# Summing a head's sixteen products by identity matmuls on TensorE for two of a block's full pairs of chunks

## Chip, cores, metric

One NeuronCore of one Trainium2 chip runs the whole program. The metric is the time on the device in microseconds, from one launch. All arithmetic of the kernel is in fp32. In the text PE is TensorE, DVE is VectorE, ACT is ScalarE, POOL is GpSimd and SP is SyncE, which issues plain DMAs.

## What is computed

Sixteen graphs share one sparse adjacency matrix of 1024 nodes (about 0.8% of its entries are ones). A node has 128 features for each graph. Four layers run one after the other: three of attention with eight heads of 16 features (L0, L2, L3), and one graph-attention layer with a single head (L1). Cut to what matters here, an attention layer is:

```
Q = (h @ Wq).reshape(B, N, NUM_HEADS, HEAD_DIM)     # 8 heads of 16
K = (h @ Wk).reshape(B, N, NUM_HEADS, HEAD_DIM)
V = (h @ Wv).reshape(B, N, NUM_HEADS, HEAD_DIM)
scores = einsum('bnhd,bmhd->bhnm', Q, K) / sqrt(HEAD_DIM)
scores = where(adj_matrix == 0, -inf, scores)
attn = softmax(scores, axis=-1)
attn_out = einsum('bhnm,bmhd->bnhd', attn, V).reshape(B, N, OUT_DIM)
x = layer_norm(h + (attn_out @ Wo + bo))
y = relu(x @ W1 + b1) @ W2 + b2
x = layer_norm(x + y)
```

The change concerns the sum over d in `scores`, the product of a query and a key over the 16 features of a head.

## The kernel before

**Sparse form.** Nodes are sorted by degree. For a set of 128 edge slots, K and V rows of the neighbours are gathered from a table in HBM, one row of each slot to a partition, 8 graphs at a time. Such a set is a chunk: 128 slots, 8 graphs x 128 features of K (`ROW` = 1024 numbers), and as many of V.

**Units, pieces, parts.** A unit is a layer, a half of the graphs (`GR` = 2) and a block of 128 nodes (`T` = 8); an attention layer has 16 units, the kernel 48 of them, and L1 has 16 of its own. A unit's chunks stand in pieces of two (full pairs) and one piece of a single mixed chunk, which is always the fourth of the unit (`MIX`). Blocks 1 to 6 have four full pairs, block 0 has five and block 7 has three. In the attention layers each piece is one part, the step of the main loop.

**The work of a part,** and its lines:

- `gathered` (L942, POOL): two indirect DMAs bring K and V rows into one of four buffers `e`.
- `products` (L954, DVE): K times the queries, elementwise, into `pr` (128 x 2048), one of four buffers.
- `exponentials` (L977, DVE): a reduction over the 16 features of each head, 128 x 2048 to 128 x 128, into `sc`; then the exponential `ex` (L981, ACT).
- `weighted` (L1005, DVE): V times `ex`, into the same `pr`. When it has read V, the gather buffer is free, and the gather four parts ahead is issued.
- `summed` (L1021, PE): matmuls with 0/1 matrices `marks` add the slots of each node into the accumulator `acc`.

When a unit is done, `divided` (L1058, L1061) divides by the sum of the exponentials, and `attention_tail` (L697 to L739) does the rest of the layer for the two halves of the graphs: transposes (L642), Wo (L706), W1 (L717), W2 (L731), the additions of the residual by the matrix `centre` (L707, L735) and two normalisations (L620, L635 on ACT). `project` (L572, L576) makes the next layer's table. `queries` (L896 to L908) makes the next unit's queries and spreads them over the slots.

**The order is written by hand.** Each engine runs its instructions in the order of the program. In step i the loop emits `products(i)`, `summed(i-2)`, a round of other work (`others`: steps of the tails, queries, loads), `exponentials(i)`, in a unit's second part also the copies of the shared queries (`shared`, on SP) and the loading of a later unit's inputs (`loaded`), a second round of `others`, `weighted(i-1)`, the gather of part i-1+4, and a third round. PSUM tiles named `ps` take turns in four banks (`bank`).

Of the kernel before, what the change touches and what calls it, by code (L numbers as in the profile page):

```python
# [17 lines left out]
AF = mybir.ActivationFunctionType  # L18
# [4 lines left out]
P = 128  # L23
D = 128
H = 8
HD = 16
# [19 lines left out]
G = B // GR  # L46
# [20 lines left out]
MIX = J  # L67
# [44 lines left out]
def of_piece(v, piece):  # L112

    a, b = piece[0][0], piece[-1][0]
    if len(piece) == 2 and a == b:
        return v[:, a : a + 1].to_broadcast([v.shape[0], 2, v.shape[2]])
    return v[:, a : b + 1 : max(b - a, 1)]
# [20 lines left out]
def sparse_path(ctx: ExitStack, tc: tile.TileContext, a: dict, out: bass.AP, flag):  # L138


    nc = tc.nc
# [6 lines left out]
    def bank(shape):  # L148
        return banks.tile(shape, F32, tag="ps", name="ps")

    ident = const.tile([P, P], F32, name="ident")
# [50 lines left out]
    def gather_buffer():  # L202
        return gathers.tile([P, max(4 * ROW, J * (ROW + G))], F32, tag="e", name="e")
# [618 lines left out]
    def exponents():  # L822
        return exps.tile([P, MOST * G * H], F32, tag="ex", name="ex")
# [3 lines left out]
    parts = []  # L827
# [7 lines left out]
    es, prs, exs, qs, qx, ofs, accums = {}, {}, {}, {}, {}, {}, {}  # L835

    def is_attention(u):
        return LAYERS[units[u][0]][1] is ATTN
# [122 lines left out]
    def exs_of(i):  # L961

        u, pieces = parts[i]
        t = units[u][2]
        c, n = PLACE[(t, *pieces[0][0])], sum(map(len, pieces))
        return exs[u][:, c : c + n, :], n

    def exponentials(i):
        u, pieces = parts[i]
        t = units[u][2]  # L970
        heads = H if is_attention(u) else 1
        sc = smalls.tile([P, es[i].shape[1], G * heads], F32, tag="sc", name="sc")
        if u not in exs:
            exs[u] = exponents()[:, : MOST * G * heads].rearrange("p (c a) -> p c a", a=G * heads)
        ex, n = exs_of(i)
        if is_attention(u):
            nc.vector.tensor_reduce(  # L977
                sc[:, :n, :], prs[i][0][:, :n, :].rearrange("p k (a d) -> p k a d", d=HD),
                mybir.AxisListType.X, ALU.add,
            )  # L980
            nc.scalar.activation(ex, sc[:, :n, :], AF.Exp, scale=1.0 / HD**0.5)  # L981
        else:
            k = 0
            for piece in pieces:
                m = k + len(piece)
                nc.vector.tensor_tensor(
                    sc[:, k:m, :], es[i][:, k:m, ROW:], of_piece(ofs[u], piece), ALU.add
                )
                k = m
            nc.vector.scalar_tensor_tensor(  # L990
                sc[:, :n, :], sc[:, :n, :], SLOPE, sc[:, :n, :], ALU.mult, ALU.max
            )
            nc.scalar.activation(ex, sc[:, :n, :], AF.Exp)
# [88 lines left out]
    def advance(gens):  # L1082
        for gen in list(gens):
            got = next(gen, "end")
            if got == "end":
                gens.remove(gen)
            elif got == "free":
                free.append(gen)
# [3 lines left out]
    def idle():  # L1092
        return slow if held[0] or not busy[0] else []

    def others():
        pace[0] += pace[1]
        while pace[0] >= 1.0:
            advance(tails)
            pace[0] -= 1.0
        while True:  # L1100
            gens = fronts or loads or idle()
            if not gens:
                break
            got = next(gens[0], "end")
            if got == "end":
                gens.pop(0)
                continue
            if got == "idle":
                advance(idle())
            break  # L1110

    with tc.manual_schedule():
        wide = [gather_buffer() for _ in range(EDGES)]
        setup, entry, weights = graph(wide), at_once(0), load_weights("L0")
        next(setup)
        next(weights)
        next(entry)
        more = [weights, load_graph_weights()]
        rest = slots()
        for i, room in enumerate(setup):  # L1120
            if i == T:
                for gen in more:
                    next(gen)
            if room == "load":
                for _ in loaded(0):
                    next(entry, None)
            elif room == "queries":
                for _ in entry:
                    pass
                for _ in queries(0):  # L1130
                    pass
            elif isinstance(room, str):
                next(rest)
            else:
                for _ in range(room):
                    next(entry, None)
        for _ in entry:
            pass
        scratch.close()
        prods = ctx.enter_context(tc.tile_pool(name="prods", bufs=4))  # L1140
        smalls = ctx.enter_context(tc.tile_pool(name="smalls", bufs=3))
        slow.append(at_leisure(1))
        second = loaded(1)
        next(second)
        for i in range(AHEAD - 1):
            gathered(i)
        nc.gpsimd.memset(wide[3], 0.0)
        gathered(AHEAD - 1)
        fronts.extend([islice(rest, 4), second] + more)
        closing, sizes = None, ()  # L1150
        begun = 0
        for i in range(len(parts) + 2):
            here = i < len(parts)
            u = parts[i][0] if here else len(units)
            if here:
                l = units[u][0]
                if i and parts[i - 1][0] != u:
                    begun = i
                    if u < T - 1:
                        fronts.append(islice(rest, 4))  # L1160
                    if l + 1 < len(LAYERS) and LAYERS[l + 1][1] is ATTN:
                        if units[u][1:] == (0, 1):
                            more = load_weights(LAYERS[l + 1][0])
                            next(more)
                            next(more)
                        if units[u][1:] == (0, 4):
                            fronts.append(more)
                if is_attention(u):
                    products(i)
            if i > 1:  # L1170
                summed(i - 2)
                done = parts[i - 2][0]
                if parts[i - 1 : i] == [] or parts[i - 1][0] != done:
                    closing = divided(done)
                    next(closing)
            others()
            if here:
                exponentials(i)
            if here and i == begun + 1:
                if is_attention(u):  # L1180
                    shared(u)
                while loads:
                    advance(loads)
                if u + 1 < len(units):
                    fronts.append(queries(u + 1))
                loads.append(loaded(u + 2))
                if u:
                    advance(loads)
            others()
            if 0 < i <= len(parts):  # L1190
                weighted(i - 1, 0)
                if not is_attention(parts[i - 1][0]):
                    others()
                    weighted(i - 1, 2)
                gathered(i - 1 + AHEAD)
                for _ in sizes:
                    pass
            if closing is not None and here:
                while any(gen not in free for gen in tails):
                    advance(tails)  # L1200
                next(closing)
                sizes, closing = closing, None
                passes = 3 if is_attention(u) else 4
                steps = STEPS if is_attention(done) else GRAPH_STEPS
                steps -= LATE[units[done][0]]
                pace[:] = 0.0, steps / (passes * sum(part[0] == u for part in parts) - 1)
            others()
            if i + 1 >= len(parts) or parts[i + 1][0] != u:

                while fronts:  # L1210
                    advance(fronts)
        while tails:
            advance(tails)
        for _ in closing:
            pass
        while tails:
            advance(tails)
# [11 lines left out]
    ps = bank([1, 1])  # L1229
# [423 lines left out]
```

## Time and profile before

| what | value |
|---|---|
| runs, us | 2286.37, 2286.7, 2300.34; median 2286.7 |
| span of the profiled execution | 2290.8 us |
| PE / DVE / ACT / POOL busy | 90 / 82 / 67 / 46% |
| reductions L977 of 128 x 2048 | 192, 438.9 us, 2286 ns each |
| `products` L954 of 128 x 2048 | 192, 439.7 us, 2290 ns each |
| exponentials L981 of 128 x 128 | 192, 61.9 us, 323 ns each |
| DMA, mean | 278 GB/s |

The first attention unit is closed at 162 us and the last at 2253 us; the units of L1 lie between 793 and 1060 us. A group of instructions is shown as: line, engine, operation, output and inputs with shapes, count, then busy us and the mean of one in ns, and after the second bar the idle time of the engine just before it and what ended that. For PE the duration of one matmul contains the time in which the next is already under way.

### The profile page before, as it was taken

The numbers are of one execution on the slowest core, as the hardware profiler recorded it, in microseconds if no ns is written. First come the engines' busy times: TensorE is split into PE (matmuls) and PEld (weight loads), VectorE is DVE, ScalarE is ACT, GpSimd is POOL, SyncE is SP. The second block draws the span as 40 slices with busy tenths as digits, with TensorE's granted clock in tenths as the row PEclk, the third lists the DMA queues.
The fourth block names the chain that finished last, engine by engine and source line by source line (L and its number), as shares of the span: only waits on it lengthen the run. The fifth ranks groups of instructions, "written<-read, shape, count | busy, mean of one in ns | idle before, by whom it ended". The sixth has DMA issues, their size and how long they took to land. (4 is left out here: it accounts for less than half of the span.)

```text
span 2290.8 us, 36572 instructions
## 1 busy us (share of the span) xinstructions
PE 2052.0 (90%) x13140; PEld 1271.6 (56%) x13140; DVE 1871.1 (82%) x1472; ACT 1530.3 (67%) x5041; POOL 1050.7 (46%) x730
## 2 busy tenths in 40 slices
PE   6479999899998999998899989999999988998987
PEld 5336666555555555554465655655655555555544
DVE  7898888588888477777988889988888887988783
ACT  3237777777776565556677777777777766776765
POOL 3355344245445278884443434333344444444540
PEclk8789999999999999999999999999999998999999
DMA  7868888678887699997998978888887877677750
GB/s 249 278 217 300 304 279 305 240 247 302 285 295 265 197 330 354 354 373 288 326 318 292 319 254 306 296 314 295 281 282 277 291 258 250 242 275 270 260 217 20
DMA packets 165197, 636.06 MB, mean 278 GB/s; under 512 B 35064, under 2 KB 37880, under 8 KB 116510
## 3 DMA queue, kind: packets, MB, share of 16 engines
q0 software_dynamic: 89216, 485.08, 59.3%
q1 hardware_dynamic: 75792, 148.57, 18.9%
q8 instruction: 105, 1.72, 0.3%
q14 instruction: 84, 0.69, 0.1%
HBM read 581.08 MB, written 92.34 MB: 294 GB/s over the span
## 5 line engine op out<-in xcount | busy, mean ns | idle before, releaser
L942 POOL DMA_INDIRECT e<-table,idx x576 | 844.2, 1466 | 1022.1 <-DVE pr L1005 796.6
L1005 DVE TENSOR_TENSOR pr<-e,ex 128x2048 f32<-128x2048 f32 (+1 forms) x320 | 661.3, 2075 | 55.9 <-ACT ex L981 32.7
L954 DVE TENSOR_TENSOR pr<-e,qr 128x2048 f32<-128x2048 f32 x192 | 439.7, 2290 | 160.3 <-DMA e<-table,idx 91.5
L1021 PE MATMUL acc<-pr,marks 128*32 128x512 f32 x2624 | 528.5, 616 | 20.3 <-DVE pr L1005 16.4
L977 DVE TENSOR_REDUCE sc<-pr 128x128 f32<-128x2048 f32 (+1 forms) x240 | 497.5, 2073 | 8.0
L620 ACT ACTIVATE z<-yps,root 128x128 f32<-128x128 f32 x888 | 319.0, 390 | 35.6 <-PE yps L735 16.8
L1021 PEld LDWEIGHTS acc<-pr,marks 128*32 128x32 f32 x2624 | 108.7, 111 | 280.9 <-issue 231.6
L635 ACT ACTIVATE z<-yps,rstd 128x128 f32<-128x128 f32 x888 | 255.0, 371 | 7.2
L731 PE MATMUL yps<-W,f 128*128 128x128 f32 x1520 | 252.6, 283 | 7.7 <-ACT f L726 1.9
L726 ACT ACTIVATE f<-ps,b 128x512 f32<-128x512 f32 x190 | 130.6, 695 | 160.4 <-PE ps L717 159.7
L731 PEld LDWEIGHTS yps<-W,f 128*128 128x128 f32 x1520 | 205.7, 193 | 51.7 <-issue 26.2
L572 PE MATMUL ps<-Wkv,xT 128*128 128x256 f32 x768 | 212.2, 417 | 20.0 <-ACT xT L648 14.4
L908 ACT COPY qr<-ps 128x512 f32<-128x512 f32 x384 | 197.1, 602 | 47.7 <-PE ps L905 47.7
L642 PE MATMUL ps<-ident,z 128*128 128x128 f32 x896 | 179.7, 300 | 41.4 <-ACT z L635 36.6
L642 PEld LDWEIGHTS ps<-ident,z 128*128 128x128 f32 x896 | 116.2, 143 | 167.7 <-ACT z L635 86.5
L717 PE MATMUL ps<-x,W 128*128 128x512 f32 x384 | 193.9, 630 | 12.5 <-ACT x L650 12.4
L620 ACT ACTIVATION_READ_ACCUMULATOR z<-yps,root 128x1 f32 x888 | 203.7, 229 | 0.0
L905 PE MATMUL ps<-q,rep 32*128 32x512 f32 x768 | 166.5, 661 | 36.4 <-ACT q L900 34.0
L572 PEld LDWEIGHTS ps<-Wkv,xT 128*128 128x128 f32 x768 | 146.5, 204 | 73.9 <-ACT qr L908 18.0
L981 ACT ACTIVATE ex<-sc 128x128 f32<-128x128 f32 (+1 forms) x240 | 76.4, 318 | 157.9 <-DVE sc L977 157.8
L576 ACT COPY kv<-ps 128x512 f32<-128x512 f32 x176 | 103.3, 593 | 108.1 <-PE ps L572 85.8
L706 PE MATMUL yps<-Wo,oT 128*128 128x128 f32 x768 | 159.9, 291 | 10.0 <-ACT oT L648 10.0
(174 smaller groups left out, 2724.2 us busy)
## 6 DMA issues: line engine op xcount, KB each, us to landing
table<-kv SPq DMA_DIRECT2D x88, 512.0 KB
kept<-xT SPq DMA_DIRECT2D x96, 256.0 KB
x<-kept SPq DMA_DIRECT2D x48, 512.0 KB
qx<-qr SPq DMA_DIRECT2D x48, 256.0 KB
e<-table,idx POOLq DMA_INDIRECT x576
table<-kv SPq DMA_DIRECT2D x32, 256.0 KB
qx<-qr SPq DMA_DIRECT2D x18, 384.0 KB
qx<-qr SPq DMA_DIRECT2D x42, 128.0 KB
```

The lines of the kernel that those rows point to most:

```text
L572: nc.tensor.matmul(ps[:, k, :], x[:, i + k, :], w[LAYERS[l][0], "Wkv"], start=True, stop=True,)
L620: nc.scalar.activation(z[:, i, :], y[:, i, :], AF.Square, scale=D**-0.5, bias=root, accum_out=total[:, i : i + 1],)
L635: nc.scalar.activation(z[:, i, :], y[:, i, :], AF.Copy, scale=rstd[:, i : i + 1])
L642: nc.tensor.transpose(ps[:, i, :], z[:, i, :], ident)
L717: nc.tensor.matmul(ps, p["W1"][:, f * P : (f + 1) * P], x1.rearrange("p g n -> p (g n)"), start=True, stop=True,)
L731: nc.tensor.matmul(ps[:, i, :], f1[:, f, i * P : (i + 1) * P], p["W2"][:, f, :], start=(f == 0), stop=False,)
L908: nc.scalar.copy(qs[u][:, j, h * GH * D : (h + 1) * GH * D], pss[j])
L942: nc.gpsimd.indirect_dma_start(out=es[i][:, k, :], out_offset=None, in_=tables[l, g][:, :], in_offset=bass.IndirectOffsetOnAxis(ap=idx[:, ...
L954: nc.vector.tensor_tensor(prs[i][0][:, :n, :], es[i][:, :n, :ROW], qx[u].rearrange("p (o c) -> p o c", o=1) if (MIX, 0) in piece else of_p ...
L977: nc.vector.tensor_reduce(sc[:, :n, :], prs[i][0][:, :n, :].rearrange("p k (a d) -> p k a d", d=HD), mybir.AxisListType.X, ALU.add,)
L1005: nc.vector.tensor_tensor(prs[i][k0 // 2][:, :m, :].rearrange("p k (a d) -> p k a d", d=d), es[i][:, k0 : k0 + m, base : base + ROW].rearr ...
L1021: nc.tensor.matmul(outs[32 * j : 32 * j + 32], marks[:, mark, :], rhss, start=(chunk == mine[0]), stop=(chunk == mine[-1]),)
```

## The change

In an attention unit, the parts at positions 1 and 4 (counted from 0), where they are full pairs, no longer reduce on DVE. `by_matmul` picks them. For such a part sixteen matmuls with the identity as stationary matrix read `pr`, each taking the numbers at one feature d of all heads (every 16th number of a row), and add them up in one PSUM tile of 128 x 128. ACT takes the exponential from there. The tile `sc` is not written for these parts. Their call of `exponentials` is emitted after the second round of `others` instead of before it.

```diff
+    def by_matmul(i):
+
+        u, (piece, *_) = parts[i]
+        if not is_attention(u) or (MIX, 0) in piece or len(piece) < 2:
+            return False
+        first = next(k for k in range(i, -1, -1) if k == 0 or parts[k - 1][0] != u)
+        return i - first in (1, 4)
+
     def exponentials(i):
...
-        if is_attention(u):
+        if by_matmul(i):
+            ps = bank([P, n, G * H])
+            terms = prs[i][0][:, :n, :].rearrange("p k (a d) -> p k a d", d=HD)
+            for d in range(HD):
+                nc.tensor.matmul(
+                    ps, ident, terms[:, :, :, d], start=(d == 0), stop=(d == HD - 1)
+                )
+            nc.scalar.activation(ex, ps, AF.Exp, scale=1.0 / HD**0.5)
+        elif is_attention(u):
             nc.vector.tensor_reduce(
...
-            if here:
+            if here and not by_matmul(i):
                 exponentials(i)
             if here and i == begun + 1:
                 if is_attention(u):
...
             others()
+            if here and by_matmul(i):
+                exponentials(i)
             if 0 < i <= len(parts):
                 weighted(i - 1, 0)
```

## The prediction

> **What bounds the kernel now.** I read the busy table first, then the sums of busy time over stretches, then single instructions in order of time.
>
> ```profile
> PE 2052.0 (90%) x13140; PEld 1271.6 (56%) x13140; DVE 1871.1 (82%) x1472; ACT 1530.3 (67%) x5041; POOL 1050.7 (46%) x730
> L942 POOL DMA_INDIRECT e<-table,idx x576 | 844.2, 1466 | 1022.1 <-DVE pr L1005 796.6
> L954 DVE TENSOR_TENSOR pr<-e,qr 128x2048 f32<-128x2048 f32 x192 | 439.7, 2290 | 160.3 <-DMA e<-table,idx 91.5
> L977 DVE TENSOR_REDUCE sc<-pr 128x128 f32<-128x2048 f32 (+1 forms) x240 | 497.5, 2073 | 8.0
> ```
>
> GpSimd waits 797 us for VectorE (L1005 frees the gather buffers), which makes VectorE look like the engine to relieve. But its own idle time names others. The stretches below lie inside L0, inside L1, over L2 and inside L3; columns are PE, weight loads, VectorE, ScalarE and GpSimd busy us, granted clock, DMA share, GB/s.
>
> ```profile
> 162.00:756.00 594.00, 545.32 (x3604) 352.74 (x3603) 489.07 (x373) 438.34 (x1488) 268.10 (x183) 0.99 0.80 279
> 790.00:1060.00 270.00, 259.50 (x1839) 145.82 (x1841) 189.24 (x239) 158.29 (x597) 190.73 (x138) 0.99 0.92 340
> 1105.00:1700.00 595.00, 559.35 (x3553) 351.73 (x3551) 521.60 (x301) 441.30 (x1410) 237.86 (x162) 0.97 0.85 295
> 1700.00:2224.00 524.00, 471.95 (x2989) 284.38 (x2986) 445.89 (x249) 371.70 (x1204) 242.54 (x165) 0.95 0.74 265
> ```
>
> TensorE is the busiest in every stretch; VectorE follows at 82, 88 and 85% in the attention layers. [...]I count spacing in the order of time (start, duration, instruction):
>
> ```profile
> 1309.57 0.61 PE L731 MATMUL yps<-W,f 128*128 128x128 f32 x4
> 1310.02 0.39 PE L735 MATMUL yps<-centre,x 128*128 128x128 f32 x2
> 1310.24 0.61 PE L731 MATMUL yps<-W,f 128*128 128x128 f32 x4
> 1310.69 0.39 PE L735 MATMUL yps<-centre,x 128*128 128x128 f32 x2
> ```
>
> The reader is to see that four instructions take 0.45 us from start to start and two take 0.22: **110 ns per 128x128 fp32 instruction**, although one is shown as 275 ns long. I count 512-column instructions at 430 ns from L717's starts in the same view (1307.65 to 1308.08). One L2 unit, 1289.45 to 1326.13 (36.7 us), then holds: 120 instructions of 128 columns (13.2 us), 16 of L905 and 24 of L572 at 215 ns (8.6), four blocks of L1021 at 1.72 (6.9), 8 of L717 (3.4) and the small sums (0.9): 33.0 us, **90% real load**. The same count over 500:700 (L0) gives 170 of 200 us (85%), over 1700:2200 (L3) 404 of 500 (81%). In L2 VectorE's waits name PE (the accumulations of L1021 21.8 us, others 15 us) ahead of the gathers (13 us); only in L3 do gathers lead (62.8 us). So TensorE sets the pace in L2 and is close behind in L0 and L3.
>
> [...]L745 issues 32 calls and shows 64 matmuls, so a call is two instructions. [...]loads overlap here, and 110 ns contains them. [...]The change reads every 16th fp32, 64 bytes apart[...]. No TensorE read of that kind is in the trace. VectorE has one (L271, 128 elements 128 bytes apart, 365 ns) against 279 ns for 128 adjacent ones (L474), some 0.7 ns more for each element.
>
> **The change, part by part.** How often: eight units of 128 rows in each of two graph groups in three attention layers; seven have two such pairs, the last (three pairs) has one. That is 15 x 2 x 3 = 90 parts, 30 a layer.
>
> *Removed:* 90 reductions at 2.286 us from VectorE, 205.7 us or 4.3 us a unit.
>
> *Added:* 90 bursts of 16 calls, 32 instructions each. At 110 ns a burst is 3.52 us; 2880 instructions are **316.8 us** on TensorE, 105.6 a layer, 6.6 a unit. Weight loads: the same 2880, inside the 110. Lower end for one instruction: 110 ns, since nothing of this form runs faster here[...]. Upper end: VectorE's extra 0.7 ns on 128 elements gives 200, rounded to a doubling, 220 ns; then the bursts are 634 us. I take 110: an fp32 element is needed only every 0.86 ns here[...]; VectorE's is an inference across engines.
>
> *ScalarE:* the exponential reads PSUM instead of SBUF. L908 and L900 read PSUM at 0.60 us for 512 columns, so 128 columns stay near the present 0.32. Between nothing and 0.1 us each, 9 us in all; ScalarE is 67% busy, nothing if so covered.
>
> *Moved:* for these parts the exponential goes behind `shared`, `loaded` and a second round of other work. Passed on SP are the copies qx<-qr (1 to 3) and one load of kept; on POOL in L0 the row gathers. They read nothing the exponential makes, so they start no later. The gather of the next part still waits for `weighted`. On ScalarE the tail's copies of that round now go ahead of the exponential; `weighted` of the next step needs it, behind one earlier `weighted` and one `products` (4.6 us), enough for a 3.5 us burst unless PE is behind. Where PE is behind, it is PE's own time, counted already.
>
> *New waits:* the burst stands in PE's queue until `products` is done. Ahead of it are an accumulation (about 1.8 us) and two rounds of other matmuls, against 2.29 us of `products`, so the wait is near nothing; from 0 to 1 us a burst, 90 us at worst. Behind it stand the tails and the next accumulation. The burst takes one of four banks until its exponential; one eviction late costs about 0.6 us, 0 to 50 us in all. Neither gain nor loss is taken for these.
>
> **The sum.** Real load a unit plus 6.6 against the present length: L0 0.855 x 39.6 + 6.6 = 40.5 (now 39.6); L2 0.90 x 37.0 + 6.6 = 39.9 (now 37.0); L3 0.81 x 37.8 + 6.6 = 37.2 (now 37.8). A perfectly packed TensorE would add 0.9, 2.9 and 0 us, x16 = 61 us: the lower bound, 2350. If every bubble stays, all 317 come on top: 2608. I take 93% packing, between L2's 90% and the 96% that L1 shows: 43.5, 42.9, 40.0 us, so +3.9, +5.9, +2.2, x16 = +192. The profiled span is 2290.8, 0.2% above the median 2286.7; 2483 of span is **2480 us** as a median. The removed 205.7 us of VectorE are worth nothing here: TensorE then covers them, and what is late next is the accumulation L1021 and whatever PE does behind a burst.
>
> **The rivals.**
> *1. Strided reads cost a doubling.* [...]Against: TensorE's slow fp32 pace. Per unit 13.2 us: 47.1, 46.5, 43.8, over 0.95 (a fuller queue) 49.6, 48.9, 46.1, so +10.0, +11.9, +8.3, x16 = +483: about 2770. Between the two, any partial penalty.
> *2. VectorE is the bound and the burst is hidden: faster.* The place is PE's idle time in the stretches above, 48.7 + 35.6 + 52.0 = 136 us, 3.0 a unit. It decides where a burst is under half of that, 1.5 us or 47 ns per instruction. For it: GpSimd's 797 us wait on VectorE, and the page's large VectorE share. Against: 110 ns spacing. The gathers' own queue is 74 to 85% busy, so I price half of the 206: 2185.
> *3. It costs as much as it gives.* L0 and L3 hide all, L2's ScalarE waits vanish: 2287 to 2310.
> *4. The change does less than it says,* if identity weights stayed loaded and each call ran as one pass: 16 x 110 = 1.76 us a burst, 3.3 a unit; with half of the 3.0 idle absorbed +1.8 x 48 = +86, still slower, 2375.
>
> **How the numbers follow.** Forecast 0.50 (its own range 2350 to 2608), rival 1 and partial penalties 0.38, rival 2 0.05, rival 3 0.03, rival 4 0.04. A measurement of this kernel tells about 1% (23 us) from no change. Faster over 1%: 0.05. Within 1%: 0.03. Slower: 0.92. The range leaves out rivals 2 to 4 and the far ends, and takes in rival 1's price: 2375 to 2790.
>
> **What will show it.** Starts of consecutive identity matmuls 110 ns apart (rival 1: nearer 220). PE near 95% busy in L2, VectorE from 88% to under 72%. VectorE's waits on PE and on the exponential grow to hundreds of us. GpSimd's wait for L1005 stays, since slots come free no sooner. L2 grows most, L3 least. I am wrong if identity matmuls are spaced under 50 ns, if VectorE stays above 85% with a shorter span, or if PE's idle time grows: then the burst's waits, not its length, are the price.

## The result and the profile after

The changed kernel takes 2782.8 us (median of 4 runs, 2777.0 to 2785.9) against 2291.6 us before: a ratio of 1.2145, interval 1.2103 to 1.2187. It is slower, as forecast, but by 491 us and not by 193; the price is that of the first rival (2770 us), not of the forecast (2480 us, at most 2608 with every idle gap kept).

The page of the changed kernel, busy table and groups (line, engine, operation, count, busy us, mean ns, then idle time before and its releaser). L988 is the identity matmul, L1021 is `weighted`, L1037 the accumulation, L991 the exponential from PSUM, L993 the reductions that remain:

```profile
PE 2628.4 (94%) x16020; PEld 1843.6 (66%) x16020; DVE 1683.7 (60%) x1382; ACT 1528.1 (55%) x5041; POOL 1029.7 (37%) x730
...
L942 POOL DMA_INDIRECT e<-table,idx x576 | 837.7, 1454 | 1514.5 <-DVE pr L1021 1283.9
L1021 DVE TENSOR_TENSOR pr<-e,ex 128x2048 f32<-128x2048 f32 (+1 forms) x320 | 666.1, 2090 | 610.3 <-ACT ex L991 492.2
L988 PE MATMUL ps<-pr,ident 128*128 128x128 f32 x2880 | 644.1, 395 | 14.2 <-DVE pr L954 10.3
...
L954 DVE TENSOR_TENSOR pr<-e,qr 128x2048 f32<-128x2048 f32 x192 | 438.8, 2285 | 229.4 <-PE acc L1037 163.2
...
L991 ACT ACTIVATE ex<-ps 128x128 f32<-128x128 f32 x90 | 24.9, 277 | 558.4 <-PE ps L988 558.4
L993 DVE TENSOR_REDUCE sc<-pr 128x128 f32<-128x2048 f32 (+1 forms) x150 | 291.7, 1945 | 5.1
```

The counts are as worked out: 2880 instructions on PE, 90 reductions gone (240 to 150). PE's busy time rose by 576 us, DVE's fell by 187. The bursts (the sixteen matmuls of a part, 32 instructions) are busy 644 us, but the span grew by 493 only: PE's idle time fell by 83 us (239 to 156), and its other instructions were busy 68 us less (1984 instead of 2052). The mean granted clock of the profiled execution was 0.979 after and 0.956 before; what that is worth in time was not tried. DVE now waits for the exponential of these parts (492 us) and ACT for the bursts (558 us), but PE itself waited for `products` only 10 us before a burst: the queue is behind because PE is full. Stretches inside L2 and L3 (columns as before):

```profile
1300.00:2050.00 750.00, 735.82 (x4430) 533.80 (x4430) 447.57 (x262) 433.01 (x1378) 220.55 (x158) 1.00 0.67 231
2050.00:2740.00 690.00, 675.24 (x4087) 477.82 (x4086) 415.24 (x238) 395.62 (x1292) 247.91 (x170) 1.00 0.60 207
```

PE is 98% busy in both, at a granted clock of 1.00, DVE 60%. One burst in order of time, on PE:

```profile
1520.84 1.88 PE L717 MATMUL ps<-x,W 128*128 128x512 f32 x4
1522.56 7.14 PE L988 MATMUL ps<-pr,ident 128*128 128x128 f32 x32
1529.63 1.91 PE L1037 MATMUL acc<-pr,marks 128*32 128x512 f32 x8
```

From its start to the next instruction's start a burst takes 7.07 us, 221 ns for each of its 32 instructions, and not 110. The mean time from one unit's closing to the next (starts of the reciprocal after each unit; in L0 from its first to its last, in the other layers from the last of the layer before to their own last) shows where it went:

| us per unit | before | after | forecast | rival 1 | adjacent reads |
|---|---|---|---|---|---|
| L0 | 39.6 | 51.9 | 43.5 | 49.6 | 45.0 |
| L1 | 19.4 | 19.3 | unchanged | unchanged | 19.0 |
| L2 | 36.8 | 47.0 | 42.9 | 48.9 | 40.9 |
| L3 | 37.4 | 46.1 | 40.0 | 46.1 | 39.7 |

The last column belongs to the first experiment.

### The profile page after: what moved, and what is told of

The parts are those of the page before. It is cut to its first block, busy times and chain, and to the rows that moved or that the text cites. A ratio compares the mean times of both kernels' runs of the same rounds, so it can differ in the third digit from the quotient of the medians.

```text
span 2784.1 us, 42319 instructions
## 1 busy us (share of the span) xinstructions
PE 2628.4 (94%) x16020; PEld 1843.6 (66%) x16020; DVE 1683.7 (60%) x1382; ACT 1528.1 (55%) x5041; POOL 1029.7 (37%) x730
## 5 line engine op out<-in xcount | busy, mean ns | idle before, releaser
L1021 DVE TENSOR_TENSOR pr<-e,ex 128x2048 f32<-128x2048 f32 (+1 forms) x320 | 666.1, 2090 | 610.3 <-ACT ex L991 492.2
L988 PE MATMUL ps<-pr,ident 128*128 128x128 f32 x2880 | 644.1, 395 | 14.2 <-DVE pr L954 10.3
L988 PEld LDWEIGHTS ps<-pr,ident 128*128 128x128 f32 x2880 | 587.5, 207 | 58.9 <-issue 11.7
L1037 PE MATMUL acc<-pr,marks 128*32 128x512 f32 x2624 | 514.1, 604 | 14.6 <-DVE pr L1021 11.4
L991 ACT ACTIVATE ex<-ps 128x128 f32<-128x128 f32 x90 | 24.9, 277 | 558.4 <-PE ps L988 558.4
L993 DVE TENSOR_REDUCE sc<-pr 128x128 f32<-128x2048 f32 (+1 forms) x150 | 291.7, 1945 | 5.1
L1037 PEld LDWEIGHTS acc<-pr,marks 128*32 128x32 f32 x2624 | 107.0, 110 | 255.3 <-issue 219.6
L572 PE MATMUL ps<-Wkv,xT 128*128 128x256 f32 x768 | 203.1, 403 | 7.0 <-ACT xT L648 4.3
L642 PE MATMUL ps<-ident,z 128*128 128x128 f32 x896 | 173.4, 295 | 12.1 <-ACT z L635 6.3
L572 PEld LDWEIGHTS ps<-Wkv,xT 128*128 128x128 f32 x768 | 140.9, 196 | 57.8 <-ACT qr L908 19.5
```

The lines of the kernel that those rows point to most:

```text
L572: nc.tensor.matmul(ps[:, k, :], x[:, i + k, :], w[LAYERS[l][0], "Wkv"], start=True, stop=True,)
L642: nc.tensor.transpose(ps[:, i, :], z[:, i, :], ident)
L988: nc.tensor.matmul(ps, ident, terms[:, :, :, d], start=(d == 0), stop=(d == HD - 1))
L993: nc.vector.tensor_reduce(sc[:, :n, :], prs[i][0][:, :n, :].rearrange("p k (a d) -> p k a d", d=HD), mybir.AxisListType.X, ALU.add,)
L1021: nc.vector.tensor_tensor(prs[i][k0 // 2][:, :m, :].rearrange("p k (a d) -> p k a d", d=d), es[i][:, k0 : k0 + m, base : base + ROW].rearr ...
L1037: nc.tensor.matmul(outs[32 * j : 32 * j + 32], marks[:, mark, :], rhss, start=(chunk == mine[0]), stop=(chunk == mine[-1]),)
```

## The experiments

Three causes could double a burst: the step of the reads (theory S), weight loads that do not overlap with the matmuls (W), sixteen additions waiting for each other on one PSUM tile (A). Beside them stood the late exponential, and the worth of the freed DVE.

**Adjacent reads.** Sizes, weights, accumulation and order stay:

```diff
-                    ps, ident, terms[:, :, :, d], start=(d == 0), stop=(d == HD - 1)
+                    ps.rearrange("p k a -> p (k a)"), ident, flat[:, d * P : (d + 1) * P],
+                    start=(d == 0), stop=(d == HD - 1),
```

> The sixteen identity matmuls of a burst read 128 adjacent numbers of pr each instead of every 16th; number, sizes, weights and the one accumulating PSUM tile stay. It sums other products than a head's sixteen, so the scores are not the reference's. Theory S (the step of 64 bytes between elements of the moving operand costs the doubling): the instructions come 110 ns apart, a burst takes 3.5 us instead of 7.1, and the time is what the forecast gave for an undoubled burst, 2480 us (2350 to 2608). Theory W (the repeated loads of the identity do not overlap with the matmuls, 110 + 110) and theory A (sixteen additions on one PSUM tile wait for each other): 221 ns, 7.1 us and 2780 us stay.

Measured: 2469.9 us, ratio 1.0824 (1.0785 to 1.0864). The group and, from the order of time, one burst:

```profile
L988 PE MATMUL ps<-pr,ident 128*128 128x128 f32 x2880 | 339.3, 276 | 9.9 <-DVE pr L954 9.9
```

```profile
1413.66 3.73 PE L988 MATMUL ps<-pr,ident 128*128 128x128 f32 x32
```

The same 2880 instructions are busy 339 us instead of 644, one is shown with 276 ns instead of 395, and a burst lasts 3.73 us. Only the addresses of the moving operand changed, so W and A fall and S stands. The time is that of the forecast's total.

**Feature-major products.** The whole computation, but DVE writes the products in the order that PE wants:

```diff
+                prs[i][0].rearrange("p k c -> p (k c)").rearrange(
+                    "p (d k a) -> p k a d", k=2, d=HD
+                ),
...
+                    ps.rearrange("p k a -> p (k a)"), ident, flat[:, d * P : (d + 1) * P],
```

> For the same parts VectorE writes the products so that one feature of all heads and both chunks lies in 128 adjacent numbers, and the matmuls read adjacent numbers; everything is computed. Theory S: bursts of 3.5 us as with adjacent reads, and the time of that run if VectorE's scattered write (256 bytes apart) is no slower than 2.29 us; if the write is slowed as L271's read is (some 0.7 ns an element, 1.4 us for 2048), VectorE has room for it and the time is at most 1% longer. Theories W and A: 2780 us.

Measured: 2479.3 us, 1.0859 (1.0818 to 1.0900). Here L955 is the scattered write and L964 the plain one:

```profile
L955 DVE TENSOR_TENSOR pr<-e,qr 128x2048 f32<-128x2048 f32 x90 | 338.9, 3765 | 190.2 <-PE acc L1048 187.1
...
L964 DVE TENSOR_TENSOR pr<-e,qr 128x2048 f32<-128x2048 f32 x102 | 232.8, 2282 | 66.2 <-DMA e<-table,idx 40.5
```

The scattered write costs 1.48 us more, 0.72 ns an element (its innermost step is 512 bytes; the expectation's 256 was wrong, its 0.7 ns was right). 90 of them are 133 us of DVE, and the time moved by 9 us against adjacent reads, inside both intervals. So this repaired form is still 8.6% slower than the kernel before.

**Which steps cost.** Two kernels read the numbers with other steps, a different one at a unit's second and fifth part; `s` is the step in elements:

```diff
+                        to, ident, flat[:, at : at + P * s - s + 1 : s],
```

> The bursts read 128 numbers with a step of 2 elements (8 bytes) at a unit's second part and of 4 elements (16 bytes) at its fifth; else as the changed kernel. It sums other products than a head's sixteen. [...]8 bytes [...]costs 110 ns an instruction, 16 bytes costs 221 already. Rival, a price that grows with the step: both between 110 and 160. Time under the first, the mean of the two kernels measured: about 2615 us.

> The same with steps of 3 elements (12 bytes) and of 8 elements (32 bytes). [...]32 bytes costs 221 ns as 16 and 64 do; 12 bytes[...] about 190. Rival, a price that grows with the step: 32 bytes well below 221, 12 bytes near 110. Time under the first about 2730 us.

Measured: 2643.7 and 2733.8 us (one run each, expected 2615 and 2730). Bursts in order of time; L993 is the second part, L1000 the fifth. Steps of 2 and 4:

```profile
1502.96 7.52 PE L1000 MATMUL ps<-pr,ident 128*128 128x128 f32 x32
...
1520.14 3.79 PE L993 MATMUL ps<-pr,ident 128*128 128x128 f32 x32
```

Steps of 3 and 8:

```profile
1515.94 5.70 PE L993 MATMUL ps<-pr,ident 128*128 128x128 f32 x32
...
1545.22 7.62 PE L1000 MATMUL ps<-pr,ident 128*128 128x128 f32 x32
```

The spacing is the duration less one instruction's own (274 to 412 ns), over 31: step 1 and 2: 112 and 113 ns; step 3: 173 (190 was expected); step 4: 229; step 8: 233; step 16: 217. From 4 elements, 16 bytes, on the price no longer grows: 229, 233 and 217 ns at 16, 32 and 64 bytes. So it does not go by distance.

What it goes by in these runs is the number of aligned stretches of 16 bytes, counted from the start of a row of `pr`, on which the numbers lie. Such a stretch is called a line below; that is a count of addresses, and how the memory is built no run shows. 128 numbers lie on 32, 64, 96 and 128 lines at steps of 1, 2, 3 and 4 or more. 113 ns for 64 lines, 173 for 96 and 217 to 233 for 128 are 1.7 to 1.8 ns a line each time. Only at step 1 is an instruction longer than that, 112 ns for 32 lines: 0.87 ns an element, called the elements' own pace below. So these runs fit one rule: the larger of 0.87 ns an element and 1.7 to 1.8 ns a line.

**Pairs and runs.**

```diff
+                        ps.rearrange("p k (b c) -> p (k b) c", c=2), ident, rows[:, :64, at : at + 2],
...
+                        ps.rearrange("p k (b c) -> p (k b) c", c=H), ident, rows[:, :, H * d : H * d + H],
```

> At a unit's second part the matmuls read pairs of adjacent numbers, 64 bytes from pair to pair; at its fifth, runs of eight adjacent numbers, 512 bytes from run to run (the order that a feature-major layout of the queries and keys would give). Other products than a head's sixteen are summed. If a line wants two reads to cost nothing, wherever the next line lies: 110 ns for both, and about 2470 us. If the jump itself costs: pairs up to 221 ns, runs near 125.

Measured: 2510.2 us (one run). L992 reads pairs, L998 runs of eight:

```profile
1410.72 4.41 PE L992 MATMUL ps<-pr,ident 128*128 128x128 f32 x32
...
1438.69 3.73 PE L998 MATMUL ps<-pr,ident 128*128 128x128 f32 x32
```

Runs of eight cost what adjacent reads do, 3.73 us a burst, although each begins 512 bytes on. The pairs' burst averages 133 ns an instruction, but no instruction has that price. The pairs of call `d` begin at element `d` (14 for the last call), and a line holds four elements, so those of calls 3, 7 and 11 lie across two lines. Calls 2, 3 and 4 of the burst above, two instructions each:

```profile
1411.18 0.38 PE L992 MATMUL ps<-pr,ident 128*128 128x128 f32 x2
...
1411.40 0.60 PE L992 MATMUL ps<-pr,ident 128*128 128x128 f32 x2
...
1411.82 0.40 PE L992 MATMUL ps<-pr,ident 128*128 128x128 f32 x2
```

Call 2 takes 0.22 us to the next start and call 3 takes 0.42, about as long as reads of one number a line (2 x 217 ns at a step of 64 bytes). In all 48 bursts it is calls 3, 7 and 11 whose spacing has a median of 202 to 233 ns; the others lie at 109 to 133. Three calls of sixteen at the full price give the average: (13 x 112 + 3 x 221) / 16 = 132 ns. So pairs took about the time of adjacent reads (112 ns) where both numbers lie on one line. The first reading of the expectation was right for both forms: the jump to the next pair or run, 64 or 512 bytes on, added nothing that shows.

**bf16.** The 90 parts' products in bf16, adjacent and with the old step of 16 (now 32 bytes):

```diff
+            half = prs[i][0].rearrange("p k c -> p (k c)").bitcast(BF16)[:, : 2 * ROW]
...
+                    ps.rearrange("p k a -> p (k a)"), ident16, half[:, d * P : (d + 1) * P],
```

> The 90 parts' products are written in bf16, feature-major, and summed by identity matmuls in bf16 from adjacent numbers: 16 instructions a burst instead of 32. It rounds these products to bf16. If the burst's length on TensorE is all that the change costs, an instruction at 55 to 110 ns gives 0.9 to 1.8 us a burst, and the time lies on the line from no sum (2230) to 3.5 us (2479): 2290 to 2355. If the scattered write of VectorE or the late exponential costs by itself: 2370 or more.

> The same in bf16 but in natural order, so that the matmuls read every 16th bf16, 32 bytes apart. It rounds these products to bf16. If what a new line costs is a fixed time per element of about 1.7 ns (221 ns for 128), an instruction takes 221 ns, a burst 3.5 us and the time is near 2470; if the price is a doubling of the form's own pace, 110 ns or less, 1.8 us and about 2350.

Measured: 2688.1 us, 1.1709 (1.1685 to 1.1734), and 2584.6 us, 1.1263 (1.1234 to 1.1292). The first is far above the 2290 to 2355 of a short burst alone and falls under "2370 or more"; the second is above both of its figures. The adjacent form, groups and two bursts in order of time:

```profile
L959 DVE TENSOR_TENSOR pr<-e,qr 128x2048 bf16<-128x2048 f32 x90 | 838.2, 9314 | 77.2 <-PE acc L1050 48.1 <-issue 15.2 <-DMA e<-table,idx 13.6
...
L1000 PE MATMUL ps<-pr,ident 128*128 128x128 bf16 x1440 | 115.7, 244 | 166.1 <-DVE pr L959 165.5 <-ACT src L604 0.3 <-ACT kv L600 0.2
...
1253.55 1.05 PE L1000 MATMUL ps<-pr,ident 128*128 128x128 bf16 x16
1271.30 1.89 PE L1000 MATMUL ps<-pr,ident 128*128 128x128 bf16 x16 [5.35 <-DVE pr L959]
```

A burst is short: 1.05 us, its 16 instructions 56 ns apart, or 1.89 us in the second one shown, before which PE had sat idle for DVE (5.35 us). But the scattered bf16 write takes 9.3 us, 3.4 ns an element more than the 2.29 us of the natural order, PE waits 166 us for it before bursts, and DVE is now the busiest engine (86%, PE 83%). GpSimd's gathers took 2307 ns each as well, against 1453 with adjacent fp32 reads. That DVE had become the bound is read from these shares and not tested; nor is why this write is so slow. One burst of the natural order:

```profile
1502.28 3.87 PE L1000 MATMUL ps<-pr,ident 128*128 128x128 bf16 x16
```

Its 16 instructions come 231 ns apart, (3.87 - 0.41) / 15. So where each number has a line of its own, an element costs 1.7 to 1.8 ns, in fp32 (217 to 233 / 128) as in bf16 (231 / 128). Against adjacent reads that is a factor of 2 in fp32 (112 ns) and of 4 in bf16 (56 ns). The time is some 100 us above adjacent fp32 reads by the ratios (1.1263 against 1.0824) with about the same burst. Over 1250 to 1750 us the granted clock is 0.95 against 0.99 there, and the accumulations (L1050, there L1038) average 642 against 598 ns; but at the 0.91 of the adjacent bf16 form they average 598 too. How much of the 100 us the clock makes, and why it was lower, was not tried.

**Worth of the freed VectorE.** No summing at all for the 90 parts:

```diff
-                nc.tensor.matmul(
-                    ps, ident, terms[:, :, :, d], start=(d == 0), stop=(d == HD - 1)
-                )
-            nc.scalar.activation(ex, ps, AF.Exp, scale=1.0 / HD**0.5)
+            nc.scalar.activation(
+                ex, prs[i][0][:, :n, : G * H], AF.Exp, scale=1.0 / HD**0.5
+            )
```

> The 90 parts are not summed at all: no reduction, no matmuls, the exponential reads the first 64 products of each chunk. It leaves out the sum over a head's features for these parts. It asks what the removed 205.7 us of VectorE would be worth if the summing cost nothing. My step (TensorE sets the pace in L2 and is close behind elsewhere): little, 2230 to 2287. Rival (VectorE is the bound): half of it or more, 2185 or less.

Measured: 2229.7 us, 0.9771 (0.9734 to 0.9808). It lies on the lower edge of my span and above the rival's: of 205.7 us a quarter, some 52 us, comes back when the burst costs nothing. The busy table shows PE as the busiest still:

```profile
PE 2018.1 (91%) x13140; PEld 1256.4 (56%) x13140; DVE 1670.3 (75%) x1382; ACT 1521.0 (68%) x5041; POOL 1019.4 (46%) x730
```

DVE falls from 82 to 75%, PE stays at 91% with its old 13140 instructions. By layer, L0 goes from 39.6 to 39.2 us a unit, L2 from 36.8 to 35.3, L3 from 37.4 to 35.6. These same PE instructions were busy 34 us less (2018 instead of 2052), and the mean granted clock of the profiled execution was 0.969 against 0.956. So part of the 52 us may have come with the clock and not from DVE's freed time; the runs do not separate the two. The other way round, bursts with adjacent reads and the reductions on DVE as well, their result thrown away:

```diff
+            nc.vector.tensor_reduce(
+                sc[:, :n, :], prs[i][0][:, :n, :].rearrange("p k (a d) -> p k a d", d=HD),
+                mybir.AxisListType.X, ALU.add,
+            )
```

> The bursts read adjacent numbers as in e_adjacent (other products than a head's sixteen are summed), and VectorE makes its 90 reductions besides, whose result is thrown away. It gives VectorE its 205.7 us back while TensorE carries bursts of 3.5 us. My step (with TensorE the bound the removed reductions are worth nothing): 2470 to 2500, as without them. Rival (they hid part of the bursts' cost): 2520 or more, up to 2470 + 206.

Measured: 2482.0 us, 1.0849 (1.0799 to 1.0899), against 1.0824 without them. Busy table and group, the reductions kept on DVE being L985:

```profile
PE 2323.7 (94%) x16020; PEld 1580.8 (64%) x16020; DVE 1873.5 (76%) x1472; ACT 1530.2 (62%) x5041; POOL 1039.1 (42%) x730
...
L985 DVE TENSOR_REDUCE sc<-pr 128x128 f32<-128x2048 f32 x90 | 205.7, 2286 | 2.9
```

DVE carries 206 us again and has room for them; what they cost, 0.0025 of the time or some 6 us, lies inside both intervals. Beside full bursts the removal is worth nothing that can be measured.

**The move alone.** The reduction stays on DVE but is emitted late:

```diff
-            ps = bank([P, n, G * H])
...
+            nc.vector.tensor_reduce(
+                sc[:, :n, :], prs[i][0][:, :n, :].rearrange("p k (a d) -> p k a d", d=HD),
+                mybir.AxisListType.X, ALU.add,
+            )
```

> The reduction stays on VectorE for all parts, but for the 90 parts it is emitted together with its exponential after the second round of other work, as the change does. It isolates the move. My step (the move costs nothing): 2265 to 2310. Rival (the exponential stands later on ScalarE, VectorE and the tails wait for it): 2330 or more.

Measured: 2285.0 us, 1.0015 (0.9995 to 1.0035): nothing.

**One burst a unit.**

```diff
-        return i - first in (1, 4)
+        return i - first == 1
```

> The changed kernel with bursts at a unit's second part alone: 48 of them at 7.1 us, 339 us of TensorE, about what 90 bursts of 3.5 us are (317), with 48 reductions off VectorE instead of 90. If time on TensorE alone sets the price: 2465 to 2500. If each burst costs by being in the way (a wait in the queues of TensorE and ScalarE), half of the whole change: about 2530 to 2540.

Measured: 2517.5 us, 1.0976 (1.0931 to 1.1022). 48 bursts are busy 345.7 us on PE, 90 adjacent ones 339.3; by the ratios (1.0976 against 1.0824) the times differ by some 35 us. It falls between the two expectations: time on TensorE sets most of the price, not all. PE's idle time in the profiled executions is 175 us here and 151 there, 24 us of it; the rest stays open.

## Why the prediction was wrong

**The step that failed** is the price of one instruction: "I take 110". That the pace of adjacent reads holds at a step of 64 bytes as well was the author's estimate; the trace before has no such read of TensorE. The term "At 110 ns a burst is 3.52 us; 2880 instructions are 316.8 us" measured 221 ns and 90 x 7.07 = 636 us, the upper end that was kept (634 us). What the runs fit in its place is 1.7 to 1.8 ns for each line (173 ns for 96 lines, 217 to 233 for 128). In that fit the element's own 0.87 ns covers half of a line's price, and two elements on a line cover all of it, as at a step of 8 bytes (113 ns). With one element to a line 0.85 ns each stay over ((221 - 112) / 128). The upper end had come from VectorE's 0.7 ns an element. That was thin evidence: L271 is one instruction, and it also writes 32 numbers where L474 writes one; that the two figures are near does not show one cause for both engines. But it was the only measurement at hand, and the figure named first gave it no weight, while the range, which ended at 2790, just held the result.

**The rest of the sum** met its total, in part by luck. With reads that cost 110 ns the time measured 2470 and, with everything computed, 2479 us, against 2480. By layer the sum was 1.5 us short in L0, 2.0 over in L2 and 0.3 over in L3, which nearly cancels: packing is not 93% everywhere. That 93% was put between L2's 90%, a count of spacings, and L1's 96%, which is a busy share (259.5 of 270 us) and so another measure. And the sum had no term for the clock: with adjacent reads PE's other instructions were busy 1979 us instead of 2052, at a mean granted clock of 0.978 against 0.956. For rival 1 the units were 2.3 short, 1.9 over and equal, which nearly cancels too: 2770 for 2783.

**A call is two instructions** in fp32, as read: the 1440 calls of the bursts are 2880 instructions, and with adjacent reads a call took 2 x 112 ns. In bf16 the same calls are 1440 instructions of 56 ns, a quarter of the time.

**TensorE as the bound** is shown for the kernel with bursts: 206 us of DVE added beside them moves nothing. For the kernel before it is shown less sharply: 206 us of DVE taken away without bursts give 52 us at most. **Rival 2** priced the free burst at 2185; even without any burst it is 2230. **Rival 3** (all hidden in L0 and L3) falls: both grew. **Rival 4** falls: 32 instructions a burst, 112 ns apart where reads are adjacent.

**The move** at nothing: right, 1.0015. **The wait of a burst for `products`**: 10 us in all, inside 0 to 90. **The exponential from PSUM**: 277 ns, cheaper than the 323 from SBUF. **The marks to look for**: the spacing near 220 was rival 1's; PE 98% and DVE 60% busy in L2, DVE's waits of hundreds of us on the exponential, L3 growing least and a PE idle time that did not grow came as said. Two were wrong. GpSimd's wait for `weighted` did not stay at 797 us but grew to 1284, with the same 576 gathers over a longer span. And it was L0 that grew most (12.3 us a unit), not L2 (10.2); why was not tried.

## What to carry to other kernels

Before work is moved to TensorE, count its real load from start-to-start spacing, and look at the addresses of the moving operand. Here the number of lines of 16 bytes that an instruction touches, at 1.7 to 1.8 ns each, gave its spacing where that was more than the elements' own pace: 173 ns for 96 lines and 217 to 233 for 128 in fp32 (own pace 112), and 231 for 128 in bf16 (own pace 56), where one step was tried. Pairs of fp32 numbers on one line took 109 to 133 ns at 64 bytes from pair to pair, and a burst of runs of eight, 512 bytes from run to run, the 3.73 us of adjacent reads. The scattered write by VectorE moved the price to that engine: 0.72 ns an element more in fp32, for which it had room here, and 3.4 ns more in bf16, which made it the busiest engine. Whether a layout that an earlier producer writes avoids both was not tried. And ask what the relieved engine is worth by leaving its work out once: here at most 52 of 206 us, less than any form of the burst cost.

## What the runs showed of the hardware

- TensorE's moving reads, from start to start of one instruction: 112 to 113 ns for 128 fp32 at steps of 4 and 8 bytes, 173 at 12, 217 to 233 at 16, 32 and 64; pairs 64 bytes apart 109 to 133 ns where each lies on one line of 16 bytes and 202 to 233 where it lies across two; for bf16, 56 adjacent and 231 at 32 bytes.
- VectorE's fp32 output with an innermost step of 512 bytes: 3765 instead of 2282 ns for 2048 elements. The same order in bf16 (256 bytes): 9314 ns, against 2288 in natural order.
- ScalarE's exponential of 128 x 128 took 277 ns from PSUM and 323 ns from SBUF.
